# Layer 1's sums of exponentials out of a column of ones in v

## The chip, the cores and the metric

The kernel runs on one NeuronCore of a Trainium2 chip. The number that counts is the device time of one execution in microseconds. A NeuronCore has a matrix engine (PE) that writes to PSUM, a vector engine (DVE), a scalar engine for pointwise functions (ACT), GpSimd (POOL), and a sync engine (SP) that here only issues transfers. Each engine works through its own instructions in order and waits for the others by semaphores. SBUF is the working memory with 128 partitions; transfers (DMA) run beside the engines.

## The reference

Two layers over four images of 32 x 32 tokens with 768 channels. Both layers begin with a group norm, end with a projection and a residual, and hold attention with 12 heads of 64 channels with a relative position bias by row and by column. In layer 1, q, k and v go through a 3 x 3 convolution per channel and a layer norm over the 64 channels of a head first. Cut to what matters here:

```python
# layer 1, per head; gains are 1 and offsets 0 in the inputs
v = layer_norm(dwconv3x3(v, w_pool_v), g_v, b_v)      # (x - mean) * rsqrt(var + eps) * g + b
attn = (q * scale) @ k.T + rel_h + rel_w
attn = softmax(attn)                                   # exp(s) / sum of exp(s) over the keys
o = attn @ v + q
out = x + o @ w_proj.T + b_proj
```

Ahead of gain and offset, a head's 64 channels of v sum to zero for each token, because their mean was taken off. So any weighted sum over tokens of the last channel is minus the sum of the same weighted sums of the 63 others. The softmax needs both the weighted sums of v and the plain sum of the exponentials.

## The kernel before, in words

**Tiling.** All is in float32. The work is cut into 8 stages, in the order image 0 and 1 through layer 0, the same two through layer 1, then images 2 and 3. A stage has 6 pairs of heads (`NC = 6`), so there are 48 pairs, of which 24 (12 to 23 and 36 to 47) belong to layer 1. A pair's two heads lie in partitions 0 to 63 and 64 to 127. A pair attends in two chunks of 512 queries (`QC`), and a chunk goes over its 1024 keys in 8 tiles of 128, in two groups of four (`g = 0` and `g = 4`).

**One group (`attend`, from line 692).** PE computes four score tiles (lines 753 and 755: q times k, and the position bias through a product with ones). ACT turns each into exponentials `e` (line 760, four buffers). DVE adds them into `acc` (lines 767 and 769), for both layers. After two yields PE multiplies the four `e` with v (line 775) into `av`, which gathers over the two groups. After the second group ACT copies `av` to `weighed` (line 710).

**Closing a chunk.** Three functions then wait in the list `rest`, and `more()` (lines 700 to 703) pops one behind each batch of scores and each batch of av of the next chunk. `sums` (line 713) multiplies ones with `acc` on PE, so that each of a head's 64 partitions holds the sum (tile `z`), copies it to `t` with ACT, and takes its inverse as exp(-ln) on ACT. `result` (line 730) refines the inverse in two DVE steps, multiplies `weighed` by it, and in layer 1 adds q with v's gain (lines 732 to 737). `finish` (line 742) adds v's bias in layer 0 and does nothing in layer 1.

**The order around it.** The order on PE, DVE, ACT and POOL is the order in which the program writes the instructions. `attend` yields 16 times per pair, once per step, and between the steps run the pieces that `at(step, piece)` has put there: the preparation of the next pairs (`plan`, lines 625 to 687), the group norms, the projections of the stage that has ended, and the mixing of weights and tokens for products that save a multiplication in eight. Pieces behind the scores and pieces behind av draw their PSUM banks from fixed lists (`behind_scores`, `behind_av`, line 112); the third bank behind av is the one that `small_bank` (line 125) also hands out, and `z` takes it too.

**Preparation in layer 1** (lines 652 to 686). `padded` is the PE product of q, k or v into a padded image; `taps` (line 524) is the convolution, nine DVE steps for each; `centre` (line 539, `ln_c`) takes off the head's mean on PE and `squares` (line 553) reduces on DVE; `norm` (line 558) multiplies by the inverse deviation on DVE, for v directly into the tile `vt` that line 775 reads; `back` (line 568, `ln_t`) transposes q and k on PE; `positions` (line 580, `rel`) makes the bias products, and `split` (line 606) parts them into `high` and the remainder in `whole` (lines 611 and 612) and starts 16 transfers on POOL's queue (line 622) that spread them into `bias`.

**Between stages.** The sums of outputs that a projection needs (`project`, line 821) are DVE steps at fixed steps; those of the last stage at 12, 10 and 6 steps before its end (line 940). After the last step lines 964 to 968 run the remaining `rest` beside the first products of the last projection. `mix_tokens` (line 296, additions of line 304) readies the tokens for a layer 0 stage, and its first products are `m4m` and `m3m`.

Of the kernel before, what the change touches and what calls it, by code (L numbers as in the profile page):

```python
# [9 lines left out]
F32 = mybir.dt.float32  # L10
F32R = mybir.dt.float32r
I32 = mybir.dt.int32
AF = mybir.ActivationFunctionType
ALU = mybir.AluOpType
# [3 lines left out]
P = 128  # L18
# [5 lines left out]
D = 64  # L24
HALF = T // 2
QC = 512
# [8 lines left out]
NSMALL = 81  # L35


IDENT, GROUP, CENTRE, HEADS, ONES = 0, P, 2 * P, 3 * P, 3 * P + 2
NCONST = 3 * P + 2 + D


LIMIT = 1e15
# [3 lines left out]
def two_layers(ctx: ExitStack, tc: tile.TileContext, keep, x_in, wqkv, wproj, rels, windows, vrow, small, const, onehot, picks, out):  # L46
# [19 lines left out]
    nc = tc.nc  # L66
# [5 lines left out]
    work = pool("work", 2)  # L72
# [52 lines left out]
    def small_bank(name):  # L125
        return ps_small.tile([P, 512], F32, tag="small", name=name)
# [13 lines left out]
    ctx.enter_context(tc.manual_schedule(engines={E.PE, E.DVE, E.Activation, E.Pool}))  # L140
    cst = fixed.tile([P, NCONST], F32, tag="cst", name="cst")
    nc.sync.dma_start(cst, const)
# [4 lines left out]
    def col(c, lo=0, hi=P):  # L147
        return sm[lo:hi, c : c + 1]
# [215 lines left out]
    seen = fixed.tile([P, 2 * len(items) * (T // QC)], F32, tag="seen", name="seen")  # L364
# [3 lines left out]
    class Pair:  # L368
# [189 lines left out]
        def norm(self, s):  # L558
            r = rsqrt(self.v, 2 * NKT, "ln")
            c = self.c[s].rearrange("p (a d) -> p a d", d=D)  # L560
            dst = c
            if s == 2:

                self.make_vt()
                dst = self.vt.rearrange("p t (j d) -> p (t j) d", d=D)
            nc.vector.tensor_tensor(dst, c, r.unsqueeze(2).to_broadcast([P, 2 * NKT, D]), ALU.mult)

        def back(self, s, h):

            ps = bank("ln_t")  # L570
            for t in range(NKT // 2):
                g = h * (NKT // 2) + t
                nc.tensor.transpose(ps[:, t * P : (t + 1) * P], self.c[s][:, g * P : (g + 1) * P], ident)
            g = LN + 2 * s
            if s == 0:
                self.put_q(ps, h, col(g), col(g + 1))
            else:
                self.put_k(ps, h, sk[:, g : g + 1], sk[:, g + 1 : g + 2])
# [111 lines left out]
    rest, found = [], ()  # L690

    def attend(pair, os):


        q, k, bias = pair.q, pair.k, pair.bias
        os.append(q)
        nonlocal found
        heads = [slice(j * D, (j + 1) * D) for j in range(2)]

        def more():  # L700
            nonlocal found
            if rest:
                found = rest.pop(0)(*found)

        for c in range(T // QC):
            cols = slice(c * QC, (c + 1) * QC)

            def copy(av):
                weighed = one.tile([P, QC], F32, tag="weighed", name="weighed")
                nc.scalar.copy(weighed, av)  # L710
                return weighed

            def sums(weighed, acc, c=c):

                z = small_bank("z")
                for j in range(2):
                    nc.tensor.matmul(  # L717
                        z[j * D : (j + 1) * D, :], cst[:, ONES : ONES + D], acc[:, j, :],
                        start=True, stop=True,
                    )  # L720
                at = 2 * (pair.i * (T // QC) + c)
                t = work.tile([P, QC], F32, tag="t", name="t", bufs=1)
                inv = work.tile([P, QC], F32, tag="inv", name="inv", bufs=1)
                nc.scalar.activation(t, z, AF.Copy, accum_out=seen[:, at : at + 1])

                nc.scalar.activation(inv, t, AF.Ln, bias=tiny)
                nc.scalar.activation(inv, inv, AF.Exp, scale=-1.0, accum_out=seen[:, at + 1 : at + 2])
                return weighed, t, inv

            def result(weighed, t, inv, cols=cols):  # L730

                nc.vector.scalar_tensor_tensor(t, t, -1.0, inv, ALU.mult, ALU.mult)
                nc.vector.scalar_tensor_tensor(inv, t, 2.0, inv, ALU.add, ALU.mult)

                if pair.layer:
                    nc.vector.tensor_tensor(inv, weighed, inv, ALU.mult)
                    nc.vector.scalar_tensor_tensor(q[:, cols], inv, col(LN + 4), q[:, cols], ALU.mult, ALU.add)
                else:
                    nc.vector.tensor_tensor(inv, weighed, inv, ALU.mult)
                return (inv,)  # L740

            def finish(inv, cols=cols):

                if not pair.layer:
                    nc.scalar.activation(q[:, cols], inv, AF.Identity, bias=col(pair.column(2)))

            for g in range(0, NKT, 4):
                es = []
                for kt, place in zip(range(g, g + 4), (None, place_b, place_c, None)):
                    keys = slice(kt * P, (kt + 1) * P)  # L750
                    ps = place.pair("s") if place else ps_a.tile([P, 2, 512], F32, tag="a", name="s")
                    for j, rows in enumerate(heads):
                        nc.tensor.matmul(ps[:, j, :], k[rows, keys], q[rows, cols], start=True, stop=False)  # L753
                    for j, rows in enumerate(heads):
                        nc.tensor.matmul(  # L755
                            ps[:, j, :], ones[rows, keys], bias[c][rows, kt // 2, :],
                            start=False, stop=True,
                        )
                    e = work.tile([P, 2, QC], F32, tag="e", name="e", bufs=4)
                    nc.scalar.activation(e, ps, AF.Exp)  # L760
                    es.append(e)
                other_work(behind_scores)
                more()
                if g == 0:
                    av = ps_av.tile([P, QC], F32, tag="av", name="av")
                    acc = work.tile([P, 2, QC], F32, tag="acc", name="acc", bufs=1)
                    nc.vector.tensor_tensor(acc, es[0], es[1], ALU.add)  # L767
                for e in es[2 * (g == 0) :]:
                    nc.vector.tensor_tensor(acc, acc, e, ALU.add)  # L769
                yield  # L770
                yield
                for t, e in enumerate(es):
                    kt = g + t
                    for j in range(2):
                        nc.tensor.matmul(  # L775
                            av[j * D : (j + 1) * D, :], pair.vt[:, kt, j * D : (j + 1) * D], e[:, j, :],
                            start=(kt == 0), stop=(kt == NKT - 1),
                        )
                other_work(behind_av)
                more()  # L780
                if g + 4 == NKT:
                    rest.extend((sums, result, finish))
                    found = (copy(av), acc)
                yield
                yield

# [148 lines left out]
    for k, stage in enumerate(stages):  # L935
        call, sums, products = project(stage, oss[k])
        first = (k + 1) * NC * n_steps
        if k + 1 == len(stages):
            at(first - 12, call)
            for r, *what in ((-12, range(5), (0,)), (-10, range(5), (1,)), (-6, (0,), (2,))):  # L940
                at(first + r, lambda sums=sums, what=what: sums(*what))
            continue
        at(first + 2, call)
        late = stages[k + 1][1]
        for r, what in ((1, (0,)), (6, (1,)), (8, (2,)), (9, (3,)), (10, (4,))) if late else ((4, (0, 1)), (5, (2,)), (6, (3, 4))):
            at(first + r, lambda sums=sums, what=what: sums(what))

        for r, n in zip((9, 11, 13, 15, 17, 19) if late else (7, 9, 11, 13, 14, 15), (2, 1) * 3):
            for _ in range(n):
                at(first + r, lambda products=products: next(products))  # L950
# [13 lines left out]
    found = rest.pop(0)(*found)  # L964
    next(products)
    for part in rest:
        found = part(*found)
# [22 lines left out]
def general(ctx: ExitStack, tc: tile.TileContext, bad, x_in, wqkv, wproj, rels, windows, vrow, small, const, onehot, picks, out):  # L990
# [16 lines left out]

    cst = sb([P, NCONST], "cst")
    nc.sync.dma_start(cst, const)
# [200 lines left out]
def _laid_out(inp):  # L1210
# [13 lines left out]
    cols = [f[f"L0_conv_b{k}"].reshape(NC, P).T for k in "qkv"]  # L1224
# [6 lines left out]
    head = np.kron(np.eye(2), np.full((D, D), 1.0 / D))  # L1231
    const = np.zeros((P, NCONST), np.float32)
    const[:, IDENT : IDENT + P] = eye
    const[:, GROUP : GROUP + P] = np.kron(np.eye(P // 4), np.full((4, 4), 0.25))
    const[:, CENTRE : CENTRE + P] = eye - head
    const[:, HEADS : HEADS + 2] = np.kron(np.eye(2), np.full((D, 1), 1.0 / D))
    const[:, ONES : ONES + D] = 1.0
    key = np.arange(T)
    onehot = np.concatenate([np.arange(S)[:, None] == key // S, np.arange(S)[:, None] == key % S])

# [36 lines left out]
```

## Time and profile before

| What | us |
|---|---|
| median of 3 runs | 3901.6 (3901.35 to 3903.21) |
| the profiled execution | 3898.63 |
| its span, first to last instruction | 3896.8 |
| PE busy in the span | 3826.2 |
| DVE busy | 2674.1 |
| ACT busy | 1849.1 |
| POOL busy | 412.1 |
| mean granted PE clock | 0.996 of full |

A profile is one execution. PE is the time in which matrix products run; PEld is the loading of weights beside it. A line of the order of time gives start and duration in us, engine, line of the kernel, operation, the output and input tiles, shapes and a count; in brackets stand the idle time of the engine just before, and what ended it. A name such as `shared` covers several tiles cut out of one buffer. "issue" is a wait for nothing that the profile shows. A matrix product of float32 shows as two records.

### The profile page before, as it was taken

Reading aid. Unit: us, or ns where it says so; the run is one execution under the profiler, and the core shown is the slowest. Engines: PE = TensorE matmul, PEld = TensorE weight load, DVE = VectorE, ACT = ScalarE, POOL = GpSimd, SP = SyncE. Lnnn points to the kernel's source line nnn. Section 1 sums busy time; section 2 is a strip of 40 time slices with the busy share of each in tenths; the row PEclk is TensorE's granted clock in tenths of the full one; section 3 lists DMA queues with packets and bytes.
Section 4 is the critical chain, followed back from the end, with each engine's and each line's share of the span. In section 5 each row is a group of like instructions: output and inputs, shape, how many; then the busy total and the mean of one; then the engine's idle time right before and its main releaser. Section 6 shows DMA issues by size and latency. Waiting matters only on the chain.

```text
span 3896.8 us, 79900 instructions
## 1 busy us (share of the span) xinstructions
PE 3826.2 (98%) x34748; PEld 1720.1 (44%) x34748; DVE 2674.1 (69%) x3088; ACT 1849.1 (47%) x2741; POOL 412.1 (11%) x776
## 2 busy tenths in 40 slices
PE   8999999999999999999899999999999999999998
PEld 3535535544344443444445445355443444434442
DVE  2566454558789987799653554454686898878885
ACT  2455434445255553456434554254553555525562
POOL 0111000110000110000010010011100010000010
PEclk9999999999999999999999999999999999999999
DMA  4344452321421213311144132522124121142123
GB/s 148 105 118 124 124 165 61 106 71 39 119 90 35 51 49 94 115 35 39 44 133 124 51 79 60 176 59 72 43 56 153 35 58 42 39 119 58 35 48 95
DMA packets 184710, 318.11 MB, mean 82 GB/s; under 512 B 24352, under 2 KB 77472, under 8 KB 184352
## 3 DMA queue, kind: packets, MB, share of 16 engines
q1 hardware_dynamic: 122912, 212.19, 17.3%
q0 software_dynamic: 61440, 100.71, 11.3%
q8 instruction: 277, 4.54, 0.5%
q14 instruction: 81, 0.66, 0.1%
HBM read 172.23 MB, written 39.91 MB: 54 GB/s over the span
## 4 chain that ended last, share of the span: by engine, by line
PE 86%; DVE 11%; issue 1%; DMA 1%; ACT 1%; SPq 0%; POOL 0%; DVEq 0%
PE qkv L131 18%; PE s L753 15%; PE av L775 15%; PE m1m L131 4%; PE m3m L131 4%; PE m4m L131 4%; PE s L755 4%; DVE shared L537 3%; PE p3p L131 3%; DVE acc L769 3%; PE p1p L131 3%; PE p4p L131 3%; PE ln_c L131 3%; PE rel L595 3%; PE z L717 2%; PE m L131 2%
## 5 line engine op out<-in xcount | busy, mean ns | idle before, releaser
L760 ACT ACTIVATE e<-s 128x1024 f32<-128x1024 f32 x768 | 776.7, 1024 | 406.2 <-PE s L755 372.8
L769 DVE TENSOR_TENSOR acc<-acc,e 128x1024 f32<-128x1024 f32 x576 | 705.6, 1225 | 182.1 <-ACT e L760 130.4
L753 PE MATMUL s<-q,k 64*128 64x512 f32 x3072 | 816.5, 608 | 4.7 <-ACT e L760 3.8
L131 PE MATMUL qkv<-xn,wqkv_t 128*64 128x512 f32 x3648 | 813.4, 595 | 4.1 <-DVE gmean L324 4.1
L537 DVE SCALAR_TENSOR_TENSOR shared<-shared,sm 128x1056 f32<-128x1056 f32 x576 | 758.6, 1317 | 15.0
L755 PE MATMUL s<-bias,ones 64*128 64x512 f32 x1536 | 615.5, 794 | 4.7 <-DMA bias<-whole 2.5
L775 PE MATMUL av<-e,vt 128*64 128x512 f32 x2624 | 593.9, 594 | 0.0
L622 POOL DMA_DIRECT2D bias<-high x384 | 204.1, 551 | 3225.9 <-ACT high L611 2988.5
L131 PEld LDWEIGHTS qkv<-xn,wqkv_t 128*64 128x64 f32 x3648 | 253.7, 137 | 487.2 <-issue 480.5
L520 ACT ACTIVATE shared<-qkv,sm 128x512 f32<-128x512 f32 (+1 forms) x288 | 129.1, 501 | 633.0 <-PE qkv L131 633.0
L753 PEld LDWEIGHTS s<-q,k 64*128 64x128 f32 x3072 | 283.8, 188 | 260.8 <-issue 214.9
L775 PEld LDWEIGHTS av<-e,vt 128*64 128x64 f32 x2624 | 184.3, 137 | 347.0 <-issue 321.9
L767 DVE TENSOR_TENSOR acc<-e 128x1024 f32<-128x1024 f32 x96 | 117.5, 1224 | 274.0 <-ACT e L760 265.4
L755 PEld LDWEIGHTS s<-bias,ones 64*128 64x128 f32 x1536 | 150.2, 188 | 193.1 <-issue 188.0
L622 POOL DMA_DIRECT2D bias<-whole x384 | 206.9, 567 | 104.3 <-DVE whole L612 96.4
L710 ACT COPY weighed<-av 128x512 f32<-128x512 f32 x96 | 56.3, 586 | 268.8 <-PE av L775 268.8
L131 PEld LDWEIGHTS ln_c<-cst,shared 128*64 128x64 f32 x2304 | 130.4, 137 | 47.5 <-issue 36.0
L595 PEld LDWEIGHTS rel<-q,rel 64*32 64x32 f32 x6144 | 111.9, 106 | 80.7 <-issue 60.6
L131 PE MATMUL ln_c<-cst,shared 128*64 128x128 f32 x2304 | 138.3, 273 | 5.5 <-ACT high L611 2.5
L131 PE MATMUL m4m<-xn,wqkv_t 128*64 128x512 f32 x528 | 122.3, 599 | 4.0 <-issue 3.0
L595 PE MATMUL rel<-q_t,rel 64*32 64x32 f32 x6144 | 123.6, 195 | 2.1 <-issue 2.1
L405 DVE TENSOR_TENSOR shared<-shared,m3m 128x512 f32<-128x512 f32 x66 | 45.4, 687 | 115.8 <-PE m3m L131 115.7
(151 smaller groups left out, 4223.5 us busy)
## 6 DMA issues: line engine op xcount, KB each, us to landing
bias<-high POOLq DMA_DIRECT2D x384, 128.0 KB, 2.8
bias<-whole POOLq DMA_DIRECT2D x384, 128.0 KB, 3.0
wqkv_t<-in_wqkv SPq DMA_DIRECT2D x78, 384.0 KB, 3.1
wqkv_t<-mixed SPq DMA_DIRECT2D x66, 384.0 KB, 3.1
wproj_t<-mixed SPq DMA_DIRECT2D x48, 384.0 KB, 3.3
wqkv_t<-in_wqkv SPq DMA_DIRECT2D x66, 192.0 KB, 2.5
xn<-in_x SPq DMA_DIRECT2D x24, 512.0 KB, 8.4
x<-in_x SPq DMA_DIRECT2D x48, 256.0 KB, 3.3
```

The costliest lines, as they stand in the source:

```text
L131: nc.tensor.matmul(ps[lo : lo + D], a[:, lo : lo + D], b, start=start, stop=stop, **kw)
L520: nc.scalar.activation(self.pad[s][:, rows, there : there + src.shape[2]], src, AF.Identity, bias=col(self.column(s)))
L537: nc.vector.scalar_tensor_tensor(y, window, tap, y, ALU.mult, ALU.add)
L595: nc.tensor.matmul(ps[lo : lo + S, k * S : (k + 1) * S].rearrange("p (b c) -> p b c", b=2), rel[rows, 2 * self.layer + i, first : first + ...
L622: nc.gpsimd.dma_start(sets, some.unsqueeze(1).to_broadcast([D // 2, 2, QC]))
L717: nc.tensor.matmul(z[j * D : (j + 1) * D, :], cst[:, ONES : ONES + D], acc[:, j, :], start=True, stop=True,)
L753: nc.tensor.matmul(ps[:, j, :], k[rows, keys], q[rows, cols], start=True, stop=False)
L755: nc.tensor.matmul(ps[:, j, :], ones[rows, keys], bias[c][rows, kt // 2, :], start=False, stop=True,)
L760: nc.scalar.activation(e, ps, AF.Exp)
L767: nc.vector.tensor_tensor(acc, es[0], es[1], ALU.add)
L769: nc.vector.tensor_tensor(acc, acc, e, ALU.add)
L775: nc.tensor.matmul(av[j * D : (j + 1) * D, :], pair.vt[:, kt, j * D : (j + 1) * D], e[:, j, :], start=(kt == 0), stop=(kt == NKT - 1),)
```

## The change

In layer 1 the last of each head's 64 channels in `vt` is overwritten with ones, by a memset behind the norm of v. Then row 63 and row 127 of `av` hold the sums of the exponentials of the two heads, and DVE no longer adds up `acc` in layer 1. `copy` starts two transfers on ACT's queue, behind ACT's copy of `av`, that spread each head's sum from its one partition over its 64 partitions, into `t`. `rest` holds `landed` (which does nothing), `sums`, `result` in place of `sums`, `result`, `finish`: sums and result of layer 1 come one pop, half a group of tiles, later. `sums` has one product with a new constant matrix (`whole`, 128 x 128) that passes 63 channels of each head through and puts minus their sum into the last; ACT copies that back into `weighed`, and then copies `t` on to `inv` to keep the running check of its size. Layer 0 keeps its additions, its `z` and its order. The constants grow by 128 columns, and the last of the output sums of the last stage moves from 6 to 4 steps before the end.

```diff
-IDENT, GROUP, CENTRE, HEADS, ONES = 0, P, 2 * P, 3 * P, 3 * P + 2
-NCONST = 3 * P + 2 + D
+IDENT, GROUP, CENTRE, HEADS, ONES, WHOLE = 0, P, 2 * P, 3 * P, 3 * P + 2, 3 * P + 2 + D
+NCONST = 4 * P + 2 + D
...
             nc.vector.tensor_tensor(dst, c, r.unsqueeze(2).to_broadcast([P, 2 * NKT, D]), ALU.mult)
+            if s == 2:
+                nc.vector.memset(dst[:, :, D - 1 :], 1.0)
...
             def copy(av):
                 weighed = one.tile([P, QC], F32, tag="weighed", name="weighed")
                 nc.scalar.copy(weighed, av)
-                return weighed
-
-            def sums(weighed, acc, c=c):
-
-                z = small_bank("z")
-                for j in range(2):
-                    nc.tensor.matmul(
-                        z[j * D : (j + 1) * D, :], cst[:, ONES : ONES + D], acc[:, j, :],
-                        start=True, stop=True,
-                    )
+                if not pair.layer:
+                    return weighed, acc
+                t = work.tile([P, QC], F32, tag="t", name="t", bufs=1)
+                for rows in heads:
+                    nc.scalar.dma_start(t[rows], weighed[rows.stop - 1 : rows.stop, :].unsqueeze(1).to_broadcast([1, D, QC]))
+                return weighed, t
+
+            def landed(*found):
+
+                return found
+
+            def sums(weighed, of, c=c):
+
+                z = small_bank("z" if not pair.layer else "whole")
                 at = 2 * (pair.i * (T // QC) + c)
-                t = work.tile([P, QC], F32, tag="t", name="t", bufs=1)
                 inv = work.tile([P, QC], F32, tag="inv", name="inv", bufs=1)
-                nc.scalar.activation(t, z, AF.Copy, accum_out=seen[:, at : at + 1])
+                if pair.layer:
+                    t = of
+                    halves(z, cst[:, WHOLE : WHOLE + P], weighed)
+                    nc.scalar.copy(weighed, z)
+                    nc.scalar.activation(inv, t, AF.Copy, accum_out=seen[:, at : at + 1])
+                else:
+                    t = work.tile([P, QC], F32, tag="t", name="t", bufs=1)
+                    for j, rows in enumerate(heads):
+                        nc.tensor.matmul(z[rows, :], cst[:, ONES : ONES + D], of[:, j, :], start=True, stop=True)
+                    nc.scalar.activation(t, z, AF.Copy, accum_out=seen[:, at : at + 1])
...
             def finish(inv, cols=cols):
 
-                if not pair.layer:
-                    nc.scalar.activation(q[:, cols], inv, AF.Identity, bias=col(pair.column(2)))
+                nc.scalar.activation(q[:, cols], inv, AF.Identity, bias=col(pair.column(2)))
...
-                    acc = work.tile([P, 2, QC], F32, tag="acc", name="acc", bufs=1)
-                    nc.vector.tensor_tensor(acc, es[0], es[1], ALU.add)
-                for e in es[2 * (g == 0) :]:
-                    nc.vector.tensor_tensor(acc, acc, e, ALU.add)
+                if not pair.layer:
+                    if g == 0:
+                        acc = work.tile([P, 2, QC], F32, tag="acc", name="acc", bufs=1)
+                        nc.vector.tensor_tensor(acc, es[0], es[1], ALU.add)
+                    for e in es[2 * (g == 0) :]:
+                        nc.vector.tensor_tensor(acc, acc, e, ALU.add)
...
-                    rest.extend((sums, result, finish))
-                    found = (copy(av), acc)
+                    rest.extend((landed, sums, result) if pair.layer else (sums, result, finish))
+                    found = copy(av)
...
-            for r, *what in ((-12, range(5), (0,)), (-10, range(5), (1,)), (-6, (0,), (2,))):
+            for r, *what in ((-12, range(5), (0,)), (-10, range(5), (1,)), (-4, (0,), (2,))):
...
+    whole = np.eye(D)
+    whole[:, -1] = -1.0
+    whole[-1, -1] = 0.0
+    const[:, WHOLE : WHOLE + P] = np.kron(np.eye(2), whole)
```

## The prediction

> **What bounds the kernel.** I read the page's busy times first, then the waits of PE, then the order of time around every PE gap longer than 0.25 us, then the groups of the operations that change.
>
> ```profile
> span 3896.8 us, 79900 instructions
> PE 3826.2 (98%) x34748; PEld 1720.1 (44%) x34748; DVE 2674.1 (69%) x3088; ACT 1849.1 (47%) x2741; POOL 412.1 (11%) x776
> ```
>
> PE is the bound: 70.6 us of the span are not PE work, and 17.3 of these are the first wait of the kernel. The change removes no PE work, so it can only win gaps, and the slow clock after them. The gaps, in order of time (start, duration, engine, line, tile, then idle before and releaser):
>
> ```profile
> 1860.46 5.21 DVE L769 TENSOR_TENSOR acc<-acc,e 128x1024 f32<-128x1024 f32 x4
> 1860.69 1.97 PE L131 MATMUL ln_c<-cst,shared 128*64 128x128 f32 x32 [2.51 <-ACT high L611]
> 1867.79 1.06 PE L573 MATMUL ln_t<-cst,shared 128*128 128x128 f32 x8 [1.70 <-DVE shared L566]
> 1873.26 0.79 PE L755 MATMUL s<-bias,ones 64*128 64x512 f32 x2 [2.19 <-DMA bias<-high]
> ...
> 1888.74 1.76 DVE L304 TENSOR_TENSOR xn<-xn 128x1536 f32<-128x1536 f32 x1
> 1890.60 4.22 PE L131 MATMUL m4m<-xn,wqkv_t 128*64 128x512 f32 x12 [3.04 <-issue]
> ...
> 1900.79 2.80 PE L131 MATMUL m3m<-xn,wqkv_t 128*64 128x512 f32 x12 [0.81 <-DVE shared L405]
> ...
> 3779.62 1.97 PE L131 MATMUL ln_c<-cst,shared 128*64 128x128 f32 x32 [2.26 <-DVE shared L537]
> 3786.72 1.06 PE L573 MATMUL ln_t<-cst,shared 128*128 128x128 f32 x8 [1.70 <-DVE shared L566]
> 3791.78 0.79 PE L755 MATMUL s<-bias,ones 64*128 64x512 f32 x2 [1.49 <-DMA bias<-whole]
> ...
> 3828.51 1.08 PE L717 MATMUL z<-acc,cst 128*64 128x512 f32 x4 [1.83 <-DVE acc L769]
> 3838.17 2.80 PE L131 MATMUL p3p<-q,wproj_t 128*64 128x512 f32 x12 [0.86 <-DVE os_sums L850]
> ```
>
> They cluster where the last pair of a run of layer 1 is prepared: no later pair gives PE products, and DVE, in order, puts 5.2 us of acc between the taps and the norm that PE waits for. The "issue" of 3.04 is also DVE: m4m needs the token sum of L304 that ends at 1890.5. Stage windows say what this costs (busy PE, PEld, DVE, ACT, POOL, clock, DMA):
>
> ```profile
> 1846.00:1906.00 60.00, 47.35 (x474) 21.09 (x472) 46.94 (x50) 29.07 (x40) 8.30 (x16) 0.89 0.19 46
> 3766.00:3798.00 32.00, 23.80 (x368) 13.02 (x368) 24.17 (x30) 18.82 (x26) 8.30 (x16) 0.84 0.29 67
> ```
>
> **What the Trainium skill says.** "TensorE: Matmul & The Clock Gate", Part 1: after an idle window PE runs at half clock for some 3.4 us of work. The trace agrees: four L753 records take 2.08 us at 3788.22 and 1.02 elsewhere. "SBUF — State Buffer", Door 1: transfers go at the rate of the ports their partitions reach, 27.2 GB/s for one. Each new transfer reads one partition; no run here shows that. "DMA: Bandwidth & Descriptors", Anatomy of one DMA: some 2 us fixed (fitted for GpSimd's queue). The bias transfers agree roughly: 128 KB in 2.8 to 3.0 us. Same page, Issuing engines are not separate DMA queues: the new transfers share engines with the bias.
>
> **The change part by part.** A group (busy, mean ns | idle before) and a row of the DMA issues (KB, us to landing):
>
> ```profile
> L769 DVE TENSOR_TENSOR acc<-acc,e 128x1024 f32<-128x1024 f32 x576 | 705.6, 1225 | 182.1 <-ACT e L760 130.4
> bias<-high POOLq DMA_DIRECT2D x384, 128.0 KB, 2.8
> ```
>
> *DVE.* Layer 1 has 24 pairs x 2 chunks = 48 chunks, each with 7 adds (one L767, six L769): 336 x 1.225 = 412 us go. The 24 memsets are of 128x16; the nearest rows (128x16, L157 to L160) take 0.17: 4 us come.
>
> *PE.* The product with the whole matrix has z's form (two of 128x64 on 512, 4 records of 1.08 together); it only moves behind av. 0; switching tile shape there instead bounds it at ±0.1 x 48 = ±5, and I take 0 because a score group pays the switch anyway.
>
> *ACT.* Per chunk one more 128x512 copy, 0.59, and two DMA issues at SP's 0.33: 1.25 x 48 = 60 us, on an engine 47% busy. The sums leave the stretch behind the scores and go behind av; there PE has 5.4 us of padded products or positions before it needs ACT. The copy of t from SBUF replaces that from PSUM. 0, except at issue. In a pair's first chunk, behind the copy of av and the two issues stand Ln, Exp and the next four exponentials, and PE's fourth score tile waits for the first of these:
>
> ```profile
> 3754.40 0.59 ACT L710 COPY weighed<-av 128x512 f32<-128x512 f32 x1 [2.54 <-PE av L775]
> 3755.68 4.29 ACT L760 ACTIVATE e<-s 128x1024 f32<-128x1024 f32 x4 [0.33 <-PE s L755]
> 3757.65 1.02 PE L753 MATMUL s<-q,k 64*128 64x512 f32 x4
> ```
>
> Now: copy to 3754.99, about 0.15 of semaphore, issues to 3755.8, Ln and Exp to 3756.35, first exponential to 3757.45: 0.2 short of a stall. Price 1 us over 24 chunks; bounds 0 to 10 (0.4 each).
>
> *Transfers.* 96 of 128 KB. By one port, 131 KB / 27.2 = 4.8, plus 2: 6.8 us (an estimate by the two pages). Bounds: 3 (the bias row) and 11.6 (the two in turn). From the copy to the end of the next av group the trace leaves 15 to 35 us nearly everywhere, 11.9 at 3754.4 and 9.0 at 3809.5. Hidden; without that cover ACT, in order, would hold the next exponentials.
>
> *Small gaps.* At 1173, 1685 and 3096 scores wait 1.16, 1.15 and 1.49 for ACT, whose Ln waits for L556, behind acc: 3.8. At 1213, 1725 and 3136 products wait 1.38, 1.36 and 1.37 for gmean, behind acc: 4.1. Four gaps of 1.44 (p1p, 1043 and like) are the norm of V waiting for ACT; they stay and take a memset each, -0.7. Gain 7.2 (3 to 7.2).
>
> *First end of layer 1 (1846 to 1906).* Without adds the norm of Q starts when ACT's Exp behind the copy of av allows, 1836.5 (it was 1839.1), and takes 2.0; four taps of V 4.8, squares of K 1.4, five taps 6.7: 1851.5 instead of 1860.5. The result, now here, waits for ACT's Exp of the sums (near 1851.4) and ends near 1854.3. K's norm waits for its Ln and Exp on ACT, behind the exponentials, at 1859.6 as before; 2.0 more is 1861.7 instead of 1867.6, and L612 1862.9. The four transfers of whole (2.2 to issue, 2.0 more to land, by 1869.07, 1871.24 and 1873.26) then land by 1867.3: 5.9. That takes in the 2.51 and 1.70, which stop; what is late next is the bias, by about 1. Less slow clock behind it: 1.0 of the 2.5 lost there (9.21 from first score to z at 1878.49, less the 2.19, against 4.56 at 1835). Then 3.04, the slow clock after it (4.04 from start to next product against 2.58) 1.46, and 0.81: 5.3. Sum 12.2; I take off 1.0, as the new transfers leave at 1864.5, among the bias's. 11 (6 to 13).
>
> *Second end (3766 to 3798).* Likewise whole lands near 3786.2, not 3791.8: 5.6, clock 0.8, less 1.0: 5.4 (2 to 8). The other gaps of both stretches, inside rel, are not behind DVE and stay.
>
> *The end.* The 1.83 before z goes, but the last sums have no cover. Copy to 3827.3, issues to 3828.1, landing at 3834.9. Then copy and read 0.80, Ln 0.72, Exp 0.63, four DVE steps 2.8, first os_sums 0.69: PE's third p3p piece starts at 3840.6 instead of 3836.28. Three more sums (2.0) and L850's 0.69 put the next p3p at 3843.4 instead of 3838.17: 5.2, and the 5.8 us PE idles from 3834.8 costs 1.8 of clock. +7 (2 to 12 by the transfer's bounds).
>
> Sum: -7.2 - 11 - 5.4 + 7 + 1 = -15.6. The profiled execution took 3898.6 (span 3896.8): 3883.0. The median stands 3.0 above it: 3901.6 - 15.6 = 3886.
>
> **Rivals.** *No difference:* the tail costs 12 and the new transfers hold the bias back by some 5 us at both ends of layer 1, so 23.6 - 8 - 12 - 1 = 3: 3898. For it: both meet an idle DMA engine's slowest kind of source. Against: bias and copy leave within 1 us of one another only there. *Slower, by issue:* if ACT needs 0.9 us per transfer, not 0.33, the first exponential comes 1.0 us late in 24 chunks, +24: 3909; it decides from 0.65 us per chunk of delay past the margin (15.6 / 24). For it: the margin of 0.2. Against: SP's rows of 0.33. *Slower, by landing:* above 15 us per transfer ACT holds the exponentials in some 30 regular chunks; at 17, some 30 x 1.7 = 50 us: 3936. Against: double the estimate. *More:* transfers of 3 us, tail +2, no collision: 25.6 - 3 = 22.6: 3879.
>
> **Numbers.** The main case 0.55 (own range 3880 to 3894), more 0.07, no difference 0.20, issue 0.10, landing 0.08. Some 0.2% (7.8 us) is what a measurement can tell from no change. Faster 0.62, same 0.20, slower 0.18. The range 3873 to 3910 leaves out landing, the worse half of issue, and the far ends of the bounds.
>
> **What would show it.** No acc in layer 1 and DVE near 2266 busy; PE's busy time falling only by clock; no gap before ln_c and ln_t at the two ends, the clock there above 0.95; m4m after 1880 without its 3 us; a new ACT wait for t's transfer only behind the last chunk, with a gap in p3p. It is wrong if ACT waits for transfers throughout, if fourth score tiles show gaps, or if the bias still lands as late as before.

## The result, and the profile after

The changed kernel takes 3919.2 us (median of 5 runs, 3914.9 to 3922.2), the kernel before, on the same chip, 3901.4 (5 runs, 3899.1 to 3903.2): a ratio of 1.0048, with a 95% interval of 1.0034 to 1.0061. It is slower by about 18 us; 3886 was forecast. The profiled execution took 3918.2.

The page of the changed kernel, busy times and the queues that matter (packets, MB, share of 16 DMA engines):

```profile
span 3916.3 us, 79560 instructions
...
PE 3833.2 (98%) x34748; PEld 1720.6 (44%) x34748; DVE 2277.1 (58%) x2776; ACT 1864.4 (48%) x2789; POOL 412.6 (11%) x776
...
q0 software_dynamic: 61440, 100.71, 11.0%
q10 hardware_dynamic: 7680, 12.59, 5.9%
```

DVE lost 397 us (2674.1 to 2277.1; 408 were forecast), so the change does what it says. Yet PE's idle time in the span rose from 70.6 us to 83.1, and its busy time by 7.0 for the same 34748 records, which is slow clock (a mean granted clock of 0.992, and 0.996 before). The new queue q10 holds the 96 transfers of the sums. It moves an eighth of the bytes of the bias queue q0, but its packets take more than half as much time on the engines. An engine-us is one microsecond of packet time on one of the 16 DMA engines: a transfer of the sums takes 5.9% x 3916.3 x 16 / 96 = 38.5 of them, a transfer of the bias of the same 128 KB 11.0% x 3916.3 x 16 / 768 = 9.0.

The waits of PE (total, times, longest; us), the answer to the gaps of before:

```profile
PE s L770 <- DMA bias<-whole: 17.7, 3, 9.2
...
PE p3p L131 <- DVE os_sums L848: 8.3, 1, 8.3
PE s L770 <- DMA bias<-high: 6.3, 1, 6.3
...
PE s L768 <- ACT k L497: 3.3, 2, 1.6
```

The waits of before for `acc`, `ln_c`, `ln_t`, `gmean` and the token sum are gone. In their place scores wait 24.0 us for `bias` (4.7 before), and the end 8.3 us for the last sums. In order of time, with the new transfers between:

```profile
1859.78 1.12 ACTq L719 DMA_DIRECT2D t<-weighed  x2
...
1861.26 2.10 POOL L625 DMA_DIRECT2D bias<-whole  x4
...
1861.78 1.13 PE L768 MATMUL s<-q,k 64*128 64x512 f32 x4 [1.64 <-ACT k L497]
...
1870.32 0.53 POOL L625 DMA_DIRECT2D bias<-high  x1 [5.93 <-DMA bias<-high]
...
1872.06 0.79 PE L770 MATMUL s<-bias,ones 64*128 64x512 f32 x2 [9.16 <-DMA bias<-whole]
...
1942.80 1.12 ACTq L719 DMA_DIRECT2D t<-weighed  x2
...
1957.41 0.79 PE L770 MATMUL s<-bias,ones 64*128 64x512 f32 x2 [6.35 <-DMA bias<-high]
...
3787.56 1.12 ACTq L719 DMA_DIRECT2D t<-weighed  x2
...
3798.20 0.80 PE L770 MATMUL s<-bias,ones 64*128 64x512 f32 x2 [7.51 <-DMA bias<-whole]
...
3836.20 1.12 ACTq L719 DMA_DIRECT2D t<-weighed  x2
...
3845.05 0.59 ACT L734 COPY weighed<-whole 128x512 f32<-128x512 f32 x1 [6.31 <-DMA t<-weighed]
...
3851.59 1.98 PE L131 MATMUL p3p<-os_sums,wproj_t 128*64 128x512 f32 x4 [8.34 <-DVE os_sums L848]
```

The pattern is there three times: two transfers of sums start on ACT's queue, and 10 to 15 us later PE still waits for a bias that POOL's queue started within some microseconds of them. In the first place POOL's own pause of 5.93 us is not the cause: the eight transfers that the waiting score tile needs had all been started by 1863.4, and the pause delays only those of the pair's second chunk. The third place, near 1957 at the step from image 1's layer 1 to image 2's layer 0, was not in the forecast at all. The fourth group is the last chunk, whose sums nothing covers. What it costs in the first two of these stretches (busy PE, PEld, DVE, ACT, POOL, clock, DMA share, GB/s), and behind them the second stretch before the change:

```profile
1846.00:1906.00 60.00, 47.30 (x268) 20.19 (x270) 25.13 (x33) 26.33 (x39) 8.31 (x16) 0.86 0.29 51
1900.00:1962.00 62.00, 54.37 (x744) 33.99 (x740) 10.72 (x15) 23.67 (x31) 8.32 (x16) 0.93 0.43 82
...
1900.00:1962.00 62.00, 60.98 (x784) 36.38 (x786) 23.48 (x28) 28.65 (x39) 8.31 (x16) 1.00 0.27 74
```

In the first one DVE fell from 46.94 to 25.13, and PE is busy for as little as before (47.35), at 0.86 of its clock instead of 0.89. In the second one PE is busy 54.37 us at 0.93 of its clock, where before it was 60.98 at full clock. The windows are fixed times and the changed kernel is some microseconds ahead when the first begins, so they show how busy the engines were and not equal work.

Which transfers fill the first wait is seen in the DMA view of the changed kernel between 1855 and 1880 (share of 16 engines in 25 us; then median us from issue to landing), the last two lines being the kernel before:

```profile
q0 software_dynamic: 1280, 2.10, 34.8%
q10 hardware_dynamic: 160, 0.26, 20.7%
...
bias<-high POOLq DMA_DIRECT2D x8, 128.0 KB, 6.2
bias<-whole POOLq DMA_DIRECT2D x8, 128.0 KB, 6.8
t<-weighed ACTq DMA_DIRECT2D x2, 128.0 KB, 8.1
...
bias<-high POOLq DMA_DIRECT2D x8, 128.0 KB, 2.7
bias<-whole POOLq DMA_DIRECT2D x8, 128.0 KB, 3.5
```

Two transfers of the sums hold 20.7% x 25 x 16 = 83 engine-us, on average 5.2 us on each of 16 engines, and the bias rows of the same window went from 2.7 and 3.5 us before to 6.2 and 6.8.

### The profile page after: what moved, and what is told of

Same layout as the page of the kernel before. It is cut to its first block, busy times and chain, and to the rows that moved or that the text cites. A ratio compares the mean times of both kernels' runs of the same rounds, so it can differ in the third digit from the quotient of the medians.

```text
span 3916.3 us, 79560 instructions
## 1 busy us (share of the span) xinstructions
PE 3833.2 (98%) x34748; PEld 1720.6 (44%) x34748; DVE 2277.1 (58%) x2776; ACT 1864.4 (48%) x2789; POOL 412.6 (11%) x776
## 4 chain that ended last, share of the span: by engine, by line
PE 93%; DVE 2%; DMA 2%; ACT 1%; issue 1%; POOL 0%; ACTq 0%; SPq 0%; DVEq 0%; POOLq 0%
PE qkv L131 20%; PE s L768 17%; PE av L792 16%; PE m4m L131 4%; PE m3m L131 4%; PE s L770 4%; PE m1m L131 4%; PE ln_c L131 3%; PE p3p L131 3%; PE rel L598 3%; PE p4p L131 3%; PE p1p L131 3%; PE m L131 2%; PE ln_t L576 1%; PE z L739 1%; PE p L131 1%
## 5 line engine op out<-in xcount | busy, mean ns | idle before, releaser
L770 PE MATMUL s<-bias,ones 64*128 64x512 f32 x1536 | 618.1, 798 | 24.1 <-DMA bias<-whole 17.7
L786 DVE TENSOR_TENSOR acc<-acc,e 128x1024 f32<-128x1024 f32 x288 | 352.8, 1225 | 121.3 <-ACT e L775 96.0
L157 DVE TENSOR_TENSOR t_ln<-r_ln 128x16 f32<-128x16 f32 x72 | 12.6, 175 | 355.1 <-ACT r_ln L155 355.1
L784 DVE TENSOR_TENSOR acc<-e 128x1024 f32<-128x1024 f32 x48 | 58.8, 1225 | 229.0 <-ACT e L775 220.4
L598 PE MATMUL rel<-q,rel 64*32 64x32 f32 x6144 | 122.5, 195 | 0.0
```

Of the source, the lines that this page charges most:

```text
L598: nc.tensor.matmul(ps[lo : lo + S, k * S : (k + 1) * S].rearrange("p (b c) -> p b c", b=2), rel[rows, 2 * self.layer + i, first : first + ...
L770: nc.tensor.matmul(ps[:, j, :], ones[rows, keys], bias[c][rows, kt // 2, :], start=False, stop=True,)
```

## Where the 19.5 us of the span are

A way to place a difference is to follow one event in both traces: here the end of the first group of av products of a chunk, named by pair and chunk (22.1 is the second chunk of pair 22). The table gives what each stretch adds to the span against before, in us; the small gaps are the sum from 13.0 to 15.0, 19.0 to 21.0 and 37.0 to 39.0. The last six rows are experiments, told below.

| kernel | small gaps | first end 22.1 to 23.1 | step to layer 0, 23.1 to 24.1 | second end 46.1 to 47.1 | tail, 47.1 to the end | elsewhere | span |
|---|---|---|---|---|---|---|---|
| forecast | -7.2 | -11 | 0 | -5.4 | +7 | +1 | -15.6 |
| changed kernel | -9.9 | +0.1 | +13.3 | +1.8 | +12.5 | +1.7 | +19.5 |
| without transfers | -10.3 | -6.5 | +5.1 | -7.8 | +6.4 | -2.2 | -15.3 |
| before with fewer additions | -10.3 | -8.5 | +0.3 | -8.3 | -0.1 | -0.3 | -27.2 |
| same bytes from 64 rows each | -9.6 | -7.2 | +7.8 | -5.7 | +7.0 | +1.5 | -6.2 |
| transfers half a group later | -8.1 | -2.5 | +10.7 | +2.6 | +18.6 | +9.7 | +30.9 |
| product at the ends | -9.9 | -6.8 | +5.3 | -5.1 | +2.4 | +4.2 | -9.9 |
| five pairs only | -10.6 | -6.7 | +0.5 | -4.9 | +3.5 | +3.5 | -14.8 |

One execution stands behind each row, and up to 3.0 us of "elsewhere" are there before layer 1 begins.

## The experiments

My theory after seeing the two traces: the additions were what PE waited for, as forecast, and their gain came; the transfers that read one partition took it back, by filling DMA engines that the bias needs. The rival: the new order (sums half a group later, one more copy on ACT) costs by itself, and the transfers are innocent. The runs were spread over several chips. Each ratio is to the kernel before on the same chip (medians of 3899.5 to 3901.4), and gains and losses are counted from there: the changed kernel is 17.8 us slower.

**The transfers taken away.** `t` is copied from `z` by ACT instead, and the constant matrix is one that spreads rows 63 and 127; the other 63 channels of layer 1 are lost.

```diff
-                for rows in heads:
-                    nc.scalar.dma_start(t[rows], weighed[rows.stop - 1 : rows.stop, :].unsqueeze(1).to_broadcast([1, D, QC]))
...
-                    nc.scalar.activation(inv, t, AF.Copy, accum_out=seen[:, at : at + 1])
+                    nc.scalar.activation(t, z, AF.Copy, accum_out=seen[:, at : at + 1])
```

> The changed kernel without its 96 transfers: the constant matrix spreads the sums over each head's rows in the one product that is there, and t is copied from it, so that weighed no longer holds the weighed values and the output of layer 1 is not the reference's. Theory 1 (the transfers are what costs: they hold up the bias transfers behind them and the last chunk): no wait for the bias above 2 us at the two ends of layer 1 and at the step to layer 0, no 8 us gap before the third p3p piece, about 3880. Theory 2 (the transfers are hidden; the relief of DVE brings less than forecast and something in the new order costs): within 5 us of the changed kernel less its last gap, about 3908.

3884.3 us, ratio to before 0.9965 (0.9951 to 0.9979). That is 15.4 us faster than before, so the transfers cost 15.4 + 17.8 = 33 us, with what they uncover at the end; the order by itself is not what made the kernel slower. PE in order of time, without transfers:

```profile
1858.10 1.13 PE L766 MATMUL s<-q,k 64*128 64x512 f32 x4 [0.43 <-ACT k L497]
...
1862.73 0.80 PE L768 MATMUL s<-bias,ones 64*128 64x512 f32 x2 [3.50 <-DMA bias<-whole]
...
1962.02 2.80 PE L131 MATMUL m1m<-shared,wqkv_t 128*64 128x512 f32 x12 [1.33 <-ACT t L733]
```

The 9.16 became 3.50, the wait near 1957 is gone. But 3.50 is not the "about 1" that the forecast left for the bias, and 5.1 us remain at the step to layer 0. At the tail 6.4 remain as well, where no transfer has to land: half of the changed kernel's 12.5 there is not the landing.

**The additions alone.** The kernel before, with one of seven additions per chunk left in layer 1, so that its sums cover two of eight tiles. Nothing else changes.

```diff
-                for e in es[2 * (g == 0) :]:
+                for e in () if pair.layer else es[2 * (g == 0) :]:
                     nc.vector.tensor_tensor(acc, acc, e, ALU.add)
```

> The kernel before with only the first of the seven additions to acc left in each chunk of layer 1, so that the sums of layer 1 are sums over two of eight tiles; 288 of 336 additions of 1.225 us are left out and nothing is added. It is the gain of the change alone. By the prediction's terms 7.9 of small gaps, 12 at the first end, 6 at the second and 1.8 before the last z: about 28 us, 3874. Theory 2: less than 12 us, above 3890.

3870.9 us, ratio 0.9929 (0.9913 to 0.9946): 28.8 us is what these six of seven additions cost the kernel before, near the 28 expected. The sum came out, its parts less so, which is in part luck: 10.3 in the small gaps (7.9 expected), 8.5 at the first end (12), 8.3 at the second (6) and 0.1 at the tail (1.8). Set beside the run without transfers, it parts the result in three: the additions gave 29 us, the new form without its transfers took back 13 of them (28.8 - 15.4), mainly at the step to layer 0 and at the tail, and the transfers took 33. Here too the scores wait 3.53 us for the bias at the first end, so this wait belongs to the order of the bias transfers: POOL starts two, sits 2.73 us, and goes on, as it did in the kernel before.

**The same transfers, other source rows.** v is all ones in layer 1 (the last DVE step of its norm compares the inverse deviation with itself instead of multiplying), so that every row of `weighed` holds the sum; the transfers bring the same 128 KB on the same queue at the same time, but read 64 partitions each.

```diff
-                    nc.scalar.dma_start(t[rows], weighed[rows.stop - 1 : rows.stop, :].unsqueeze(1).to_broadcast([1, D, QC]))
+                    nc.scalar.dma_start(t[rows], weighed[rows, :])
```

> The changed kernel with v of layer 1 all ones and with transfers of the same number, size, queue and place that read all 64 rows of a head instead of spreading one row, so that the output of layer 1 is not the reference's. If the slow part is the one partition that each transfer reads (one port): landing near 3 us instead of 7.9, no wait for the bias above 2 us, about 3883. If it is the added bytes on the shared engines, whatever their source: landing near 8 and about 3915.

3890.8 us, ratio 0.9976 (0.9969 to 0.9983). The queue and its row of the issues in the DMA view:

```profile
q10 hardware_dynamic: 7680, 12.59, 1.3%
...
t<-weighed ACTq DMA_DIRECT2D x96, 128.0 KB, 2.4
```

Landing is 2.4 us instead of 7.9 (the median of all 96 in the changed kernel), and a transfer holds 1.3% x 3890.6 x 16 / 96 = 8.4 engine-us instead of 38.5. In the stretch of the first end the bias lands in 3.6 and 3.8 us, where it took 6.2 and 6.8 in the changed kernel and takes 2.7 and 3.1 without transfers. The bias waits are 3.51, 1.99 and 0.71; the first is above the 2 that were expected, but it is there without transfers too. The time lies 9 us below the kernel before. So 27 of the 33 us come from reading one partition 64 times instead of 64 partitions once, and some 6 from there being transfers at all, among them the two waits of 1.6 for k at the ends, where k's last step stands on ACT behind the two issues; they do not move with the landing, and are 0.43 without transfers.

**The transfers half a group later.** They start in `landed`, behind the next group's exponentials, where no bias is on its way.

```diff
-            def landed(*found):
-                return found
+            def landed(weighed):
+                t = work.tile([P, QC], F32, tag="t", name="t", bufs=1)
+                for rows in heads:
+                    nc.scalar.dma_start(t[rows], weighed[rows.stop - 1 : rows.stop, :].unsqueeze(1).to_broadcast([1, D, QC]))
+                return weighed, t
```

> The changed kernel with the transfers started half a group later, in the function that was empty, behind the next scores and so behind the bias transfers that those scores wait for. If the new transfers hold the bias back by lying ahead of it: the waits of 9.2, 6.4 and 7.5 us for the bias fall below 2 and the wait of scores for k (1.6) goes; ACT waits for the landing in the short chunks at the ends instead, some 4 us each, and the last chunk stays: about 3895. If the bias is late for another reason (the issue on POOL, the order of ACT): the waits stay above 5 us and the time within 5 us of 3919.

3928.6 us, ratio 1.0076 (1.0059 to 1.0093): a miss of more than 30 us. The collision went as expected, the gain did not come. PE's waits, and one short chunk in order of time:

```profile
PE s L768 <- ACT e L775: 21.7, 19, 4.7
...
PE s L770 <- DMA bias<-whole: 4.6, 2, 3.6
```

```profile
3803.79 1.12 ACTq L723 DMA_DIRECT2D t<-weighed  x2
...
3812.65 0.59 ACT L734 COPY weighed<-whole 128x512 f32<-128x512 f32 x1 [7.84 <-DMA t<-weighed]
...
3816.32 2.08 PE L768 MATMUL s<-q,k 64*128 64x512 f32 x4 [4.67 <-ACT e L775]
```

The bias waits fell from 24.0 to 6.1 us. But ACT now waits 7.84 for the landing in a chunk that has no preparation beside it, the next exponentials stand behind it, and PE waits 4.67 and goes on at half clock (2.08 for four records, 1.13 elsewhere). That happens three times, and at the step to layer 0 PE waits 5.22 us (at 1929.93) for a copy that stands on ACT behind such a landing, so that stretch stays at +10.7. In 16 more chunks PE waits about half a microsecond for the exponentials, and there too ACT has first waited for the landing, as at 1153.75 (7.83 us) ahead of PE's 0.47 at 1160.13: ACT waits for it 23 times, 168 us in all, and twice, 10 us, in the changed kernel. This is the mechanism of the rival "slower, by landing", with a landing of some 8 us and less cover, which the changed kernel hardly shows: its wait for `e` is 1.3 us in all.

**A product in place of the transfer, at the ends.** PE spreads the row with one more constant matrix, in `landed`. In chunks 22.1, 23.1, 46.1, 47.0 and 47.1; all others keep their transfers.

```diff
+    const[D - 1, SPREAD : SPREAD + D] = 1.0
+    const[P - 1, SPREAD + D : SPREAD + P] = 1.0
...
-                for rows in heads:
+                for rows in () if by_product else heads:
...
+                if by_product:
+                    z = small_bank("spread")
+                    halves(z, cst[:, SPREAD : SPREAD + P], weighed)
+                    at = 2 * (pair.i * (T // QC) + c)
+                    nc.scalar.activation(t, z, AF.Copy, accum_out=seen[:, at : at + 1])
+                return weighed, t
```

> The changed kernel with the spreading done by a second product on PE (a constant matrix that copies row 63 and row 127 over each head's rows), in the function that was empty, for five chunks only: the second of pairs 22, 23 and 46 and both of pair 47. All other chunks keep their transfers. If the loss is where these transfers meet the bias, and the last chunk: no wait for the bias above 4 us, no 8 us gap in the last projection, five products of 0.9 us where PE has idle time, and the other 43 chunks cost next to nothing: about 3884, faster than the kernel before. If the transfers cost in every chunk: above 3895.

3887.5 us, ratio 0.9963 (0.9949 to 0.9976): faster than both kernels. PE in order of time:

```profile
1867.54 0.80 PE L782 MATMUL s<-bias,ones 64*128 64x512 f32 x2 [3.41 <-DMA bias<-whole]
...
3780.06 0.51 PE L782 MATMUL s<-bias,ones 64*128 64x512 f32 x2 [0.98 <-DMA bias<-high]
...
3815.95 1.08 PE L136 MATMUL spread<-weighed,cst 128*64 128x512 f32 x4 [0.69 <-ACT weighed L720]
...
3826.35 1.08 PE L136 MATMUL p3p<-os_sums,wproj_t 128*64 128x512 f32 x4 [1.59 <-DVE os_sums L860]
```

Ten transfers of 96 hold nearly all of the damage: this run is 12.8 us faster than before where the changed kernel is 17.8 slower, 31 us of the 33. The other 86 are hidden, as forecast.

**The same product in the last chunk alone, and in all 48.**

```diff
-    return (i, c) in ((22, 1), (23, 1), (46, 1), (47, 0), (47, 1))
+    return (i, c) == (47, 1)
```

> The same for the last chunk of all alone. It measures the tail: the 10.7 us that the last stretch is longer than before should fall to 1 to 3, so about 3910, while the three waits for the bias stay at 6 to 9 us. If the tail is long for its later sums, not for the landing: within 3 us of 3919.

3912.5 us, ratio 1.0031 (1.0019 to 1.0043), 12 us above before, some 6 less than the changed kernel. The p3p wait of 8.34 is 1.59 here, while the bias waits of 9.27, 6.28 and 4.11 stay. This prices the uncovered last transfer apart from the collisions.

```diff
-    return (i, c) in ((22, 1), (23, 1), (46, 1), (47, 0), (47, 1))
+    return True
```

> The same for all 48 chunks, no transfers at all. The 43 products more than in the version for five chunks lie where PE has no idle time: 0.9 each, 39 us, about 3920; the waits for the bias as without transfers. If PE had slack behind the scores: about 3885.

3916.8 us, ratio 1.0044 (1.0028 to 1.0059). Here 48 products of 1.08 us are on PE, which is the bound, and the 43 more than in the version for five chunks cost 29 us net of the transfers they replace (39 were expected); PE is busy 3861.0 us (3833.2 in the changed kernel): a transfer that is covered is cheaper than a product, one that is not covered is dearer.

**Only where it is wanted.** If the additions cost only at certain pairs, the new form is wanted only there.

```diff
+def ones_in_v(i):
+    return i in (14, 20, 22, 38, 46)
...
-            if s == 2:
+            if s == 2 and ones_in_v(self.i):
                 nc.vector.memset(dst[:, :, D - 1 :], 1.0)
...
-                if not pair.layer:
+                if not ones_in_v(pair.i):
                     if g == 0:
                         acc = work.tile([P, 2, QC], F32, tag="acc", name="acc", bufs=1)
...
-                    rest.extend((landed, sums, result) if pair.layer else (sums, result, finish))
+                    rest.extend((landed, sums, result) if ones_in_v(pair.i) else (sums, result, finish))
```

> The column of ones only in the pairs 14, 20, 22, 38 and 46, where the additions of the kernel before made PE wait; their chunks keep the transfers, but for the second chunk of 22 and of 46, where a second product spreads the sums. All other pairs of layer 1 add as before, close in the old order, and the last output sums stand at 6 steps from the end again. Theory (bias held back by slow transfers beside it, an uncovered last transfer, and a changed order behind pair 23): the three groups of small gaps give 3.4 us each as in the changed kernel, the first end 1.5 to 3.4 and the second 6.0 to 8.4 (what the runs with spreading by PE and with fewer additions gave there), nothing is lost at the step to layer 0 nor at the end: 18 to 22 us below the kernel before, near 3880. If instead something that every chunk of the new form brings were the cost, the gain would still be near this, since only 10 of 48 chunks have it; if the additions at the first and second end were not what PE waited for, only the 10 us of the small gaps would come, 3890.

3882.8 us (5 runs, 3878.7 to 3883.8) against 3899.5 of before, ratio 0.9952 (0.9938 to 0.9966): the fastest median of the kernels that leave nothing out, though its interval overlaps that of the product at the ends. The gain of 17 us is just short of the 18 to 22 expected. Of PE's waits, three lines that changed:

```profile
PE s L787 <- DMA bias<-whole: 5.3, 3, 3.4
...
PE z L755 <- DVE acc L803: 3.5, 1, 3.5
...
PE m3m L140 <- DVE shared L414: 1.8, 1, 1.8
```

The loss at the step to layer 0 is gone (+0.5), since pair 23 is in the old form: so the 5 us that stayed there without transfers belong to that pair's new form. Of these, 1.33 at `m1m` and 1.08 at a `p3p` are seen as waits of the run without transfers; the rest was not parted further. Expected was nothing lost at the end; 3.5 us were: the last `z` waits 3.5 for `acc` and not 1.83, which is 1.7 of them, and slow clock behind that longer wait covers the rest: `z` and the next p4p take 1.98 and 4.90 us, where before they took 1.08 and 2.75.

## Why the prediction was wrong

The step that failed is the price of the collision. At the first end of layer 1 it reads "I take off 1.0, as the new transfers leave at 1864.5, among the bias's", it is repeated as "less 1.0" at the second end, and everywhere else it is nothing, as bias and copy leave within 1 us of one another "only there". Measured as the changed kernel less the run without transfers, what the transfers cost is 6.6 us at the first end, 9.6 at the second (1.2 of each is k's later start, below), and 8.2 at a third place, the step to layer 0. The collision was seen and put at the wrong size: I had a price for the new transfer's landing (6.8 us) and none for the time it holds on the engines it shares. The wait for the bias became 9.16, 7.51 and 6.35 us, each followed by slow clock, and the first end gave +0.1 instead of -11, the second +1.8 instead of -5.4. The second term that was put at nothing is the new form itself without its transfers, 13 us. The gain of fewer additions, in sum, and that the regular chunks hide their transfers, were right.

Point by point:

- **DVE** fell to 2277 us (2266 forecast). **The small gaps** gave 9.9 us: right in kind, and above the forecast's own range of 3 to 7.2.
- **The first end without collision.** The forecast had `whole` ready near L612's 1862.9; its counterpart L615 starts at 1857.21, earlier than that. The step "what is late next is the bias, by about 1" was short too: it is 3.5 us without any new transfer, as the pause of 2.73 on POOL stays. Without transfers, 6.5 us were to be had, and 8.5 from fewer additions alone, not 12.2.
- **The step to layer 0** had no term: the list of places where bias and sums leave together, "only there" at the two ends, missed the one at 1942.8. The trace before shows it: the copy ends at 1945.91 and the bias starts at 1947.15, just outside the 1 us that the list asked for, while the transfer took 7.9. That is +13.3: some 8 from transfers (13.3 - 5.1) and 5 from pair 23's new form.
- **The tail** was half understood: +7 forecast, all for the landing, and +12.5 from 47.1 on, of which 1.9 come before the last group of av. The uncovered landing is there: the two issues took 1.12 us and not 0.66; from the first issue to ACT's copy 8.85 passed (7.5 forecast); and PE went on at half clock (1.98 for four records of p3p, 1.08 in the run with the product at the ends). But it is worth 6.1; the other 6.4 stay without transfers and had no term. They are 1.4 before the last group of av, about 1 in waits for the last sums, and some 4 of slow clock behind these. Behind the same wait of 1.32 us twelve records of p3p took 5.39 us without transfers and 2.79 with the product at the ends, so the clock behind the waits is not set by their length alone. What in the new form makes the waits, its later sums or the output sum that was moved, was not parted.
- **The issues on ACT** cost 0.56 us each in such a pair, between the forecast 0.33 and the rival's 0.9 (the first of two takes 0.47, the second 0.61), and the fourth score tiles show nearly no gap. What they do hold back is k at the two ends, 1.64 each instead of 0.43.
- **The rivals.** "No difference" had the right two causes, with 5 us at each of two places, and came nearest; a third place, more at each, and the cost of the new form take it to 3919. The rivals by issue and by landing hardly occur in the changed kernel: beside the last chunk ACT waits for a landing once, 3.90 us in chunk 47.0, and PE 0.74 behind it. So it became slower by none of the paths that were given to "slower".

Of what the prediction took from the Trainium skill, two places bear on the result. "DMA: Bandwidth & Descriptors", Issuing engines are not separate DMA queues: transfers share the DMA engines whoever starts them. The traces agree: the bias on POOL's queue slowed from 2.7 to 6.2 us beside two transfers on ACT's, and only to 3.6 beside two with 64 source rows, which hold 8.4 engine-us each instead of 38.5. "SBUF — State Buffer", Door 1: the rate of one partition's port led to an estimate of 6.8 us; the measured median is 7.9 (6.3 to 11.8), and 2.4 with 64 source partitions.

## What to carry to other kernels

Price a new transfer twice: by its landing for the one who waits for it, and by the engine time it takes from every transfer beside it; here 128 KB out of one partition took 38.5 engine-us against 9.0 for the bias. Then list every place where it is under way together with a transfer that the bound engine waits for, over its whole landing and not only where both start at once, and use another way in just those. A gain that sits in a few places is best taken there alone: five pairs of 24 gave 17 us, all 24 lost 18.

## What the hardware showed that I had not expected

- A transfer that reads one partition is slow for itself (7.9 us to land against 2.4) and slow for others: two of them put on average 5.2 us of packet time on each of the 16 DMA engines and held another queue's 128 KB transfers to 6.2 and 6.8 us. Whether it is the one partition or the 64-fold reading of the same 2 KB in it, and whether they block inside an engine or at the memory's port, was not tried.
- Two transfers started one behind the other on ACT's queue take 1.12 us of ACT's order, where the median start on SP's queue is 0.33.
